# Second layer of an adaptive mixture kernel: the last four blocks in two sets of two, low-rank stages between shared experts, routed gates behind the fold product

## The chip, the cores and the metric

The kernel runs on one core of a Trainium2 chip. Its engines work side by side and wait for each other by semaphores: TensorE (PE) multiplies matrices into PSUM, VectorE (DVE) does elementwise work, ScalarE (ACT) does activation functions, GpSimd (POOL) here only memsets and broadcasts, SyncE (SP) issues DMAs. PEld is TensorE's loading of weights. The metric is the device time of one execution in microseconds, the lower the better. The kernel before takes 972.35 us (median of three runs, 971.81 to 973.3).

## The reference

Input `x` is 32 batches of 128 tokens of width 128, all in fp32. Two layers follow, each of the form `x = x + ffn(cond(x))`. Layer 0 (a mixture of four conditioned experts, then eight gated experts of width 512) is not touched here. Layer 1 is:

```
shared = sum_e (silu(x s_w1[e]) * (x s_w3[e])) s_w2[e] / 2          # 2 experts, width 256
s      = sigmoid([x, cond] W_router);  the two highest get gates, normalized
routed = sum_e gelu(x r_w1[e]) r_w2[e] * gate[:, e]                 # 8 experts, width 128, exact gelu
c      = (shared + routed) / 4
x      = x + gelu_tanh((c U1) V1 + b1) (U2 V2) + b2                 # rank 32, width 512
```

Only `c U1` of rank 32 is needed of `c`. The kernel therefore multiplies `s_w2` and `r_w2` with `U1` once, into twelve matrices of 128x32 called `fold` (with the factors 1/8 and 1/4), and never forms `c`.

## The kernel before

Tokens lie in 8 blocks of 512 (`TB`), with the 128 features on the partitions (`xT`, in layer 1 `x1T`). Layer 1 takes the blocks in two halves of four (`sb` 0 and 1, `SB = 4`). Its work is a list of units, each with an up and a down function:

- `("s", sb, k)`, four per half, one for each 128 columns of the shared experts: `sh_up` makes a gate and an up product per block (`by_columns`, line 233, in four column strips of 32), a silu on ACT (line 639) and a multiply on DVE (line 640); `sh_down` adds the fold product.
- `("r", sb, e)`, eight per half: `r_up` spreads the gate of expert e over the partitions on POOL (`spread`, line 634), makes the product `ur` per block, a gelu (line 873) and the multiply with the gate (line 874); `r_down` adds the fold product.
- `("l", sb, c)`, four per half: `low_up` multiplies the 32 rows of `pT` with 128 columns of `V1` (line 891, four row strips of 32, one per block) and takes the tanh gelu with bias (line 892); `low_down` multiplies with `U2`.

`into` (line 838) does the fold and `U2` products: block j of four goes into partitions 32 j to 32 j + 31 of one PSUM tile, so that four products with 32 columns of weights run side by side in column strips. All shared and routed folds of a half add up in one PSUM tile, `p_ps`; `low_in` copies it to `pT` (line 882). `low_out` copies `q_ps` (line 902), multiplies with `V2` (line 906), adds bias and `x1T` on DVE (line 908) and stores blocks in turn through the queues of SP and ACT (line 910).

PSUM has six rotating matmul buffers (`mm_tile`) and two for sums (`y_tile`), each one tile of 128x512 fp32. A `work` buffer `h` with three copies holds the activated values of a unit.

`pipelined` sets the order of the program: the up function of the next unit comes ahead of the down function of the present one, and `after` adds side work behind certain units. In the list, all eight s units come first, then the r units of the first half, two r units of the second half, the first three l units of the first half, the other six r units, the last l unit of the first half, and the four l units of the second half. The framework that builds the kernel may still move instructions of an engine against the program's order where it takes them to be ready earlier; waits and buffers are placed by it.

The router's gates of four blocks are transposed and go through DRAM (`gates_to_dram`, the transpose at line 555). `gate_rows` (line 863) reads them back into one partition in 32, 4 DMAs of 16 KB per half, from where POOL broadcasts.

Of the kernel before, what the change touches and what calls it, by code (L numbers as in the profile page):

```python
# [32 lines left out]
F32 = mybir.dt.float32  # L33
I32 = mybir.dt.int32
AF = mybir.ActivationFunctionType
ALU = mybir.AluOpType
AX = mybir.AxisListType

P = 128
B, S, D = 32, 128, 128  # L40
BB = 4
TB = BB * S
NB = B // BB
SB = 4
NS = NB // SB
NT = B * S // P
H = 512
NC = H // P
E0, EF, E1 = 4, 8, 8
# [43 lines left out]
AT32, NCOLS32 = columns(COLS32)  # L93
# [5 lines left out]
def adaln_ffn(  # L99
# [3 lines left out]
    nc = tc.nc  # L103
    V = nc.vector

    cpool = ctx.enter_context(tc.tile_pool(name="const", bufs=1))
    wpool = ctx.enter_context(tc.tile_pool(name="weights", bufs=1))
    apool = ctx.enter_context(tc.tile_pool(name="acts", bufs=1))
    work = ctx.enter_context(tc.tile_pool(name="work", bufs=2))
# [3 lines left out]
    def mm_tile(name):  # L113
        return psum.tile([P, TB], F32, tag="mm", name=name, bufs=6)

    def y_tile(name):
        return psum.tile([P, TB], F32, tag="y", name=name, bufs=2)

    def const(shape, name, dtype=F32):
        return cpool.tile(shape, dtype, tag=name, name=name)  # L120
# [3 lines left out]
    par32 = const([P, NCOLS32], "par32")  # L124
    rows = const([P, NROW], "rows")
# [11 lines left out]
    ident = const([P, P], "ident")  # L137
# [17 lines left out]
    for to, w in zip(downs_t, (s_w2, r_w2[: E1 // 2], r_w2[E1 // 2 :])):  # L155
        n = w.shape[0]
        nc.sync.dma_start(out=to.rearrange("p (e f) -> p e f", e=n), in_=w.rearrange("e d f -> d e f"))

    def col(name, i=0, n=1):
        return par[:, AT[name].start + i : AT[name].start + i + n]  # L160
# [67 lines left out]
    def by_columns(ps, w, x, n):  # L228


        for at in range(0, P, n):
            own = slice(at, at + n)
            nc.tensor.matmul(ps[own, :], lhsT=w[:, own], rhs=x, start=True, stop=True)  # L233

# [307 lines left out]
    def of_sb(t, sb):  # L544

        return t[:, sb * SB * BB : (sb + 1) * SB * BB, :]
# [4 lines left out]
    def gates_to_dram(kind, sb):  # L551

        gates, name = held.pop((kind, sb)), f"{kind}g{sb}"
        ps = mm_tile(f"{name}_ps")
        nc.tensor.transpose(ps[:, :P], gates.rearrange("p e b -> p (e b)"), ident)
        t = work.tile([P, P], F32, tag="gsb", name=f"{name}_sb", bufs=1)
        V.tensor_copy(t, ps[:, :P])
        d = dram.tile([P, P], F32, tag=name, name=name)
        nc.sync.dma_start(out=d, in_=t)
        in_dram[kind, sb] = d.rearrange("(g k b) t -> k g (b t)", g=2, k=4)  # L560

    def ffn_logits(sb):

# [31 lines left out]
    def fetch_rows(blk):  # L595

        sb, j = divmod(blk, SB)
        t = work.tile([P, 2, TB], F32, tag="gT", name=f"fgT{blk}")
        for k in range(4):
            nc.sync.dma_start(  # L600
                out=t[32 * k : 32 * k + 1, :, :], in_=in_dram["f", sb][k : k + 1, :, j * TB : (j + 1) * TB]
            )
        return t

# [26 lines left out]
    def spread(row, name):  # L631

        bc = work.tile([P, TB], F32, tag="bc", name=name, bufs=4)
        nc.gpsimd.partition_broadcast(bc, row)  # L634
        return bc

    def glu(ps_gate, ps_up, h, name):
        s = work.tile([P, TB], F32, tag="sg", name=name, bufs=4)
        nc.scalar.activation(s, ps_gate, AF.Silu)  # L639
        V.tensor_tensor(h, s, ps_up, ALU.mult)  # L640

    l1 = const([P, NT, E1], "l1")

# [126 lines left out]
    def l1_scores(sb):  # L770
        at = split(of_sb(l1, sb))
        V.tensor_tensor(at, logits("l1", par[:, AT["r1x"]], xT, sb)[:, :, :, :E1], split(of_sb(tl, sb)), ALU.add)
        nc.scalar.activation(of_sb(l1, sb), of_sb(l1, sb), AF.Sigmoid)

    def after_ffn(blk, e):

# [53 lines left out]

    low_p = {}

    def into(y, w, h, first, last):

        for j in range(SB):
            nc.tensor.matmul(y[32 * j : 32 * (j + 1), :], lhsT=w, rhs=h[:, j, :], start=first, stop=last)  # L838

    def sh_up(sb, k):  # L840
        e, c = divmod(k, 2)
        h = work.tile([P, SB, TB], F32, tag="h", name=f"hs_{sb}_{k}", bufs=3)
        for j in range(SB):
            x = x1T[SB * sb + j]
            g, u = mm_tile(f"g1_{sb}_{k}_{j}"), mm_tile(f"u1_{sb}_{k}_{j}")
            by_columns(g, sws_t[0][:, e, c, :], x, 32)
            by_columns(u, sws_t[1][:, e, c, :], x, 32)
            glu(g, u, h[:, j, :], f"s1_{sb}_{k}_{j}")
        return h

    def sh_down(sb, k, h):
        if k == 0:
            low_p[sb] = y_tile(f"p_ps{sb}")
        into(low_p[sb], fold[:, k, :], h, k == 0, False)


    grows = [
        wpool.tile([P, 2, SB * TB], F32, tag=tag, name=f"grows{sb}") for sb, tag in enumerate(("wg", "wu"))
    ]

    def gate_rows(sb):
        for k in range(4):
            nc.sync.dma_start(out=grows[sb][32 * k : 32 * k + 1, :, :], in_=in_dram["r", sb][k : k + 1, :, :])

    def r_up(sb, e):
        h = work.tile([P, SB, TB], F32, tag="h", name=f"hr_{sb}_{e}", bufs=3)
        g, k = divmod(e, 4)
        for j in range(SB):
            gate = spread(grows[sb][32 * k : 32 * k + 1, g, j * TB : (j + 1) * TB], f"rg_{sb}_{e}_{j}")
            ps = mm_tile(f"ur_{sb}_{e}_{j}")  # L870
            by_columns(ps, rw1_t[:, e, :], x1T[SB * sb + j], 32)
            a = work.tile([P, TB], F32, tag="sg", name=f"ar_{sb}_{e}_{j}", bufs=4)
            nc.scalar.activation(a, ps, AF.Gelu)  # L873
            V.tensor_tensor(h[:, j, :], a, gate, ALU.mult)  # L874
        return h

    def r_down(sb, e, h):
        into(low_p[sb], fold[:, 2 * 2 + e, :], h, False, e == E1 - 1)

    def low_in(sb):  # L880
        t = work.tile([P, TB], F32, tag="pT", name=f"pT{sb}", bufs=1)
        V.tensor_copy(t, low_p[sb])
        held["p", sb] = t

    def low_up(sb, c):
        h = work.tile([P, SB, TB], F32, tag="h", name=f"hl_{sb}_{c}", bufs=3)
        at = AT32["v1"].start + c * P
        for j in range(SB):
            ps = mm_tile(f"ul_{sb}_{c}_{j}")
            own = slice(32 * j, 32 * (j + 1))  # L890
            nc.tensor.matmul(ps, lhsT=par32[own, at : at + P], rhs=held["p", sb][own, :], start=True, stop=True)  # L891
            nc.scalar.activation(h[:, j, :], ps, AF.Gelu_apprx_tanh, bias=col("b1", c))
        return h

    def low_down(sb, c, h):
        if c == 0:
            held["q", sb] = y_tile(f"q_ps{sb}")
        into(held["q", sb], col("u2", c * 32, 32), h, c == 0, c == NC - 1)

    def low_out(sb):  # L900
        q = work.tile([P, TB], F32, tag="lgT", name=f"qT{sb}", bufs=1)
        V.tensor_copy(q, held["q", sb])
        for j in range(SB):
            ps = mm_tile(f"o_ps{sb}_{j}")
            own = slice(32 * j, 32 * (j + 1))
            nc.tensor.matmul(ps, lhsT=par32[own, AT32["v2"]], rhs=q[own, :], start=True, stop=True)  # L906
            t = work.tile([P, TB], F32, tag="fin", name=f"fin{sb}_{j}", bufs=4)
            V.scalar_tensor_tensor(t, ps, col("b2"), x1T[SB * sb + j], ALU.add, ALU.add)
            queue = nc.sync if j % 2 == 0 else nc.scalar
            queue.dma_start(out=out[SB * sb + j], in_=t)  # L910


    STAGES = {"f": (ffn_up, ffn_down), "s": (sh_up, sh_down), "r": (r_up, r_down), "l": (low_up, low_down)}
    units = [("f", blk, e) for blk, e in ffn_units]
    units += [("s", sb, k) for sb in range(NS) for k in range(4)]
    units += [("r", 0, e) for e in range(E1)]
    units += [("r", 1, 0), ("r", 1, 1)]
    units += [("l", 0, c) for c in range(NC - 1)]
    units += [("r", 1, e) for e in range(2, E1)]

    units += [("l", 0, NC - 1)]
    units += [("l", 1, c) for c in range(NC)]

    def after(kind, sb, i):
        if kind == "f":
            after_ffn(sb, i)
        if (kind, sb, i) == ("s", 0, 0):
            gate_rows(0)
            while rest:
                rest.pop(0)()  # L930

        if (kind, sb, i) == ("s", 0, 1):
            logits_ahead("l1", par[:, AT["r1x"]], xT, 1)
        if (kind, sb, i) == ("s", 0, 2):
            l1_scores(1)
        if (kind, sb, i) == ("s", 0, 3):
            route(1)
        if (kind, sb, i) == ("s", 1, 1):
            gates_to_dram("r", 1)
            gate_rows(1)  # L940
        if kind == "r" and i == E1 - 1:
            low_in(sb)
        if (kind, sb, i) == ("l", 0, NC - 1):
            low_out(0)

    def unit_up(kind, *at):
        return STAGES[kind][0](*at)
# [2 lines left out]
        STAGES[kind][1](*at)  # L950

    pipelined(units, unit_up, unit_down, after)
    low_out(1)


# [77 lines left out]
```

## Time and profile before

The profiled execution took 972.82 us, of which the span is 971.0 us.

| stage of the span, us | what runs | PE busy | ACT busy | DVE busy | POOL busy |
|---|---|---|---|---|---|
| 802.00 to 812.50 | first s unit and the end of layer 0 | 10.50 | 2.97 | 5.00 | 3.09 |
| 812.50 to 868.60 | s units of both halves, router of the second | 56.10 | 22.22 | 32.04 | 0.00 |
| 868.60 to 911.60 | ten r units | 43.00 | 24.41 | 36.03 | 39.43 |
| 911.60 to 918.50 | first three l units of the first half | 6.90 | 6.87 | 1.46 | 2.78 |
| 918.50 to 944.40 | six r units of the second half | 25.90 | 16.87 | 22.41 | 21.47 |
| 944.40 to 965.20 | five l units, both outputs | 19.61 | 13.13 | 6.29 | 0.00 |
| 965.20 to 971.00 | last sums and stores | 0.00 | 0.00 | 2.69 | 0.00 |

In the profile a line of a time line gives start, duration, engine, source line, operation, output and inputs, shapes, a count of merged instructions, and in brackets the idle time ahead with what ended it. An fp32 matmul has two records, so x8 stands for four matmuls. Where a matmul's start waits on one strip, the records of the strips beside it go on, so busy time of PE includes some waiting.

### The profile page before, as it was taken

To read this page: it belongs to the slowest core of one execution; us is meant where nothing else is said; L and a number is where in the kernel's file an instruction comes from. 1 tells how busy PE (TensorE), PEld (TensorE's weight loads), DVE (VectorE), ACT (ScalarE), POOL (GpSimd) and SP (SyncE) were. 2 spreads that over 40 slices of the span, in tenths; PEclk is the share of its full clock that TensorE was granted. 3 is DMA by queue.
4 is the path that set the end of the run, shared out by engine and by line. 5 is a ranking of instruction groups with operands and counts; after the bars stand their busy time and mean duration, and the time that the engine had idled before them with its cause. 6 is when DMAs were issued, how large, how long until landed. Compare 5 with 4: busy or idle time off the path is not lost.

```text
span 971.0 us, 15510 instructions
## 1 busy us (share of the span) xinstructions
PE 957.0 (99%) x5966; PEld 446.9 (46%) x5966; DVE 630.1 (65%) x1130; ACT 345.0 (36%) x615; POOL 142.4 (15%) x150
## 2 busy tenths in 40 slices
PE   7999999999999999999999999999999999999997
PEld 3588984444444444444444444444444443333342
DVE  3444565767866776685676887567667655648593
ACT  5455544223322322232232332223223223335764
POOL 0000001210101011010101011010100001009680
PEclk9999999999999999999999999999999999999999
DMA  9745650000000000000000000000000000000002
GB/s 319 237 133 154 209 187 24 5 1 4 1 1 1 1 1 1 1 1 1 1 2 1 1 2 4 1 1 1 1 1 1 1 2 2 2 7 1 1 2 87
DMA packets 19043, 34.05 MB, mean 35 GB/s; under 512 B 1729, under 2 KB 9921, under 8 KB 18945
## 3 DMA queue, kind: packets, MB, share of 16 engines
q1 hardware_dynamic: 18096, 31.43, 10.6%
q10 hardware_dynamic: 864, 1.52, 0.4%
q8 instruction: 52, 0.85, 0.4%
q14 instruction: 31, 0.25, 0.1%
HBM read 30.59 MB, written 2.36 MB: 34 GB/s over the span
## 4 chain that ended last, share of the span: by engine, by line
PE 85%; DVE 0%; DVEq 0%; issue 0%
PE g L233 26%; PE u L233 25%; PE ya L721 11%; PE yb L721 9%; PE ur L233 6%; PE p_ps L838 2%; PE ul L891 1%; PE us L257 1%; PE ys L268 1%; PE q_ps L838 1%; PE y L510 0%; PE u L494 0%; PE fold_ps L244 0%; PE o_ps L906 0%; PE lg_ps L526 0%; PE l_ps L526 0%
## 5 line engine op out<-in xcount | busy, mean ns | idle before, releaser
L639 ACT ACTIVATE sf<-g 128x512 f32<-128x512 f32 x256 | 152.7, 597 | 435.2 <-PE g L233 421.3
L640 DVE TENSOR_TENSOR hf<-sf,u 128x512 f32<-128x512 f32 x256 | 174.8, 685 | 183.2 <-PE u L233 182.1
L233 PE MATMUL g<-c0all,wg_t 128*64 128x512 f32 x1024 | 263.5, 593 | 0.0
L233 PE MATMUL u<-cg,wu_t 128*64 128x512 f32 x1024 | 263.1, 592 | 0.0
L634 POOL PARTITION_BROADCAST fg<-fgT x64 | 72.4, 1140 | 657.5 <-DVE cg L682 494.4
L233 PEld LDWEIGHTS u<-cg,wu_t 128*64 128x64 f32 x1024 | 73.6, 137 | 146.2 <-issue 127.6
L233 PEld LDWEIGHTS g<-c0all,wg_t 128*64 128x64 f32 x1024 | 72.9, 137 | 121.3 <-issue 107.1
L721 PE MATMUL ya<-t,wd_t 128*64 128x256 f32 x512 | 121.0, 379 | 0.0
L634 POOL PARTITION_BROADCAST rg<-grows x64 | 67.6, 1184 | 143.8 <-DVE hr L874 75.5
L874 DVE TENSOR_TENSOR hr<-ar,rg 128x512 f32<-128x512 f32 x64 | 60.7, 995 | 15.9 <-ACT ar L873 15.9
L721 PEld LDWEIGHTS ya<-t,wd_t 128*64 128x64 f32 x512 | 70.1, 137 | 0.0
L497 ACT ACTIVATE h<-u,w 128x256 f32<-128x256 f32 (+3 forms) x136 | 50.3, 429 | 54.3 <-PE u L494 54.3
L721 PE MATMUL yb<-hf,a_sum 128*64 128x256 f32 x512 | 66.1, 379 | 0.0
L721 PE MATMUL ya<-hf,wd_t 128*64 128x256 f32 x256 | 65.8, 379 | 0.0
L721 PE MATMUL ya<-t,a_sum 128*64 128x256 f32 x256 | 65.7, 379 | 0.0
L701 DVE TENSOR_TENSOR hf<-hf 128x512 f32<-128x512 f32 x64 | 63.0, 984 | 2.2
L233 PE MATMUL ur<-xall,rw_t 128*32 128x512 f32 x512 | 58.4, 592 | 0.0
L721 PEld LDWEIGHTS ya<-hf,wd_t 128*64 128x64 f32 x256 | 35.0, 137 | 46.1 <-issue 36.8
L510 PE MATMUL y<-h,w 128*128 128x256 f32 (+3 forms) x272 | 53.1, 338 | 1.0 <-DVE t L513 1.0
L494 PE MATMUL u<-x,w 128*128 128x256 f32 (+3 forms) x272 | 53.0, 338 | 1.1 <-DVEq L475 1.1
L494 PEld LDWEIGHTS u<-x,w 128*128 128x128 f32 x272 | 45.3, 190 | 5.7 <-ACT h L497 1.3
L873 ACT ACTIVATE ar<-ur 128x512 f32<-128x512 f32 x64 | 37.9, 598 | 27.6 <-PE ur L233 27.3
(211 smaller groups left out, 918.6 us busy)
## 6 DMA issues: line engine op xcount, KB each, us to landing
w<-in_experts SPq DMA_DIRECT2D x36, 514.5 KB
xall<-in_x SPq DMA_DIRECT2D x8, 256.0 KB
wg_t<-in_w_gate SPq DMA_DIRECT2D x8, 256.0 KB
wu_t<-in_w_up SPq DMA_DIRECT2D x8, 256.0 KB
wd_t<-in_w_down SPq DMA_DIRECT2D x8, 256.0 KB
out<-fin SPq DMA_DIRECT2D x4, 256.0 KB
out<-fin ACTq DMA_DIRECT2D x4, 256.0 KB
downs<-in_r_w SPq DMA_DIRECT2D x2, 256.0 KB
```

Of the source, the lines that this page charges most:

```text
L233: nc.tensor.matmul(ps[own, :], lhsT=w[:, own], rhs=x, start=True, stop=True)
L494: nc.tensor.matmul(ps[c][:, :m, :n], lhsT=w1, rhs=x[:, :m, :n], start=True, stop=True)
L497: nc.scalar.activation(h[:, c, :m, :n], ps[c][:, :m, :n], AF.Gelu_apprx_tanh, bias=bias)
L510: nc.tensor.matmul(y[:, :m, :n], lhsT=w2, rhs=h[:, c, :m, :n], start=(c == 0), stop=(c == NC - 1))
L634: nc.gpsimd.partition_broadcast(bc, row)
L639: nc.scalar.activation(s, ps_gate, AF.Silu)
L640: V.tensor_tensor(h, s, ps_up, ALU.mult)
L701: V.tensor_tensor(b12, b12, b11, ALU.subtract)
L721: nc.tensor.matmul(y[half, n], lhsT=w[:, c, :], rhs=h[:, c, :], start=first, stop=(e == EF - 1 and last))
L838: nc.tensor.matmul(y[32 * j : 32 * (j + 1), :], lhsT=w, rhs=h[:, j, :], start=first, stop=last)
L873: nc.scalar.activation(a, ps, AF.Gelu)
L874: V.tensor_tensor(h[:, j, :], a, gate, ALU.mult)
```

## The change

It touches layer 1 alone.

- The blocks now form three groups: blocks 0 to 3 in four strips of 512 tokens as before, blocks 4 and 5, and blocks 6 and 7. A group of two blocks is cut into four strips of 256 tokens for the folds and the low-rank stages; the shared and routed up-products keep 512 columns.
- A routed unit of a group of two takes two experts. The gate is no longer multiplied into the activated values. The fold product of one expert goes into a PSUM tile of its own (one half of a tile for each of the two experts), DVE multiplies it with the gate and adds it to `low_p` in SBUF, which begins as the copy of the shared experts' sum.
- The gates come by DMA from DRAM already broadcast to 32 partitions per strip, for all eight experts (`gate_rows`: 4 DMAs of 512 KB and 8 of 256 KB); POOL broadcasts nothing more in layer 1.
- New order: s and r units of group 0; for group 1 s, s, l, l, s, s, l, l with the l units of group 0, then its four r units; the same for group 2 with the l units of group 1; then an empty unit and the l units of group 2. The output of a group comes behind the first r unit of the next.
- Matmuls in strips of 32 and ACT's instructions of layer 1 are pinned behind the instruction that the program has ahead of them on their engine. `table` issues a 1x1 activation that loads the next function's table.
- The last output: for the odd strips `x1T` is added by an identity product, issued ahead, and ACT adds the bias; DVE takes the even strips. Four stores of 128x256 follow, three on SP and one on ACT.
- The gate transpose and `gate_rows` of the second half come behind the second r unit; the sigmoid of the second half's router comes behind the last silu of group 0.

```diff
             own = slice(at, at + n)
-            nc.tensor.matmul(ps[own, :], lhsT=w[:, own], rhs=x, start=True, stop=True)
+            mm = nc.tensor.matmul(ps[own, :], lhsT=w[:, own], rhs=x, start=True, stop=True)
+            if n < 64:
+                tc.keep_in_program_order(mm)
...
+    GROUPS = ((0, 4, TB), (4, 2, TB // 2), (6, 2, TB // 2))
+    def in_order(inst):
+        tc.keep_in_program_order(inst)
+    tiny = const([1, 1], "tiny")
+    def table(func):
+        if held.get("table") != func:
+            in_order(nc.scalar.activation(tiny, ones[:1, :1], func))
+            held["table"] = func
...
+    def into(y, w, strips, first, last):
+        for j, h in enumerate(strips):
+            in_order(nc.tensor.matmul(y[32 * j : 32 * (j + 1)], lhsT=w, rhs=h, start=first, stop=last))
+    def strips_of(h, group):
+        n = GROUPS[group][2]
+        return [h[:, b, at : at + n] for b in range(h.shape[1]) for at in range(0, TB, n)]
...
+    def sh_down(group, k, h):
+        _, n, size = GROUPS[group]
+        if k == 0:
+            held["shared", group] = y_tile(f"p_ps{group}")[:, :size]
+        y = held["shared", group]
+        into(y, fold[:, k, :], strips_of(h[:, :n, :], group), k == 0, k == 3)
+        if k == 3:
+            low_p[group] = work.tile([P, 2, TB], F32, tag="gT", name=f"pT{group}")[:, 0, :size]
+            V.tensor_copy(low_p[group], y)
...
     def gate_rows(sb):
-        for k in range(4):
-            nc.sync.dma_start(out=grows[sb][32 * k : 32 * k + 1, :, :], in_=in_dram["r", sb][k : k + 1, :, :])
+        rows = in_dram["r", sb]
+        for group in (0,) if sb == 0 else (1, 2):
+            n = GROUPS[group][2]
+            for j in range(SB):
+                at = (max(group, 1) - 1) * SB * n + j * n
+                to = gates_t[sb][32 * j : 32 * (j + 1)]
+                if group > 0:
+                    to = to.rearrange("p e (g t) -> p e g t", g=2)[:, :, group - 1, :]
+                nc.sync.dma_start(out=to, in_=rows[:, at : at + n].partition_broadcast(32))
+    def r_up(group, i):
+        table(AF.Gelu)
+        h = work.tile([P, SB, TB], F32, tag="h", name=f"hr_{group}_{i}", bufs=3)
+        pieces = [(e, b) for e in experts_of(group, i) for b in blocks(group)]
+        for at, (e, b) in enumerate(pieces):
+            ps = mm_tile(f"ur_{b}_{e}")
+            by_columns(ps, rw1_t[:, e, :], x1T[b], 32)
+            in_order(nc.scalar.activation(h[:, at, :], ps, AF.Gelu))
+        return h
+    def r_down(group, i, h):
+        _, n, size = GROUPS[group]
+        ys = y_tile(f"py_{group}_{i}")
+        for at, e in enumerate(experts_of(group, i)):
+            own = h[:, at * n : (at + 1) * n, :]
+            y = ys[:, at * size : (at + 1) * size]
+            into(y, fold[:, 2 * 2 + e, :], strips_of(own, group), True, True)
+            t = work.tile([P, TB], F32, tag="sg", name=f"pg_{group}_{e}", bufs=4)[:, :size]
+            V.tensor_tensor(t, y, gate_of_strips(e, group), ALU.mult)
+            V.tensor_tensor(low_p[group], low_p[group], t, ALU.add)
+    def by_rows(ps, w, t, j, first=True):
+        own = slice(32 * j, 32 * (j + 1))
+        in_order(nc.tensor.matmul(ps, lhsT=par32[own, w], rhs=t[own, :], start=first, stop=True))
...
+    def out_begin():
+        for j in (1, 3):
+            b, at = strip(2, j)
+            held["o", j] = mm_tile(f"o_x{b}")[:, : TB // 2]
+            in_order(nc.tensor.matmul(held["o", j], lhsT=ident, rhs=x1T[b][:, at], start=True, stop=False))
+    def out_end():
+        fins = {b: work.tile([P, TB], F32, tag="fin", name=f"fin{b}", bufs=4) for b in blocks(2)}
         for j in range(SB):
+            b, at = strip(2, j)
+            t = fins[b][:, at]
+            ps = held["o", j] if j % 2 else mm_tile(f"o_ps{b}")[:, : TB // 2]
+            by_rows(ps, AT32["v2"], held["qT", 2], j, first=j % 2 == 0)
+            if j % 2 == 0:
+                V.scalar_tensor_tensor(t, ps, col("b2"), x1T[b][:, at], ALU.add, ALU.add)
+            else:
+                in_order(nc.scalar.activation(t, ps, AF.Identity, bias=col("b2")))
+        for j in (0, 2, 3, 1):
+            b, at = strip(2, j)
+            queue = nc.scalar if j == 1 else nc.sync
+            queue.dma_start(out=out[b][:, at], in_=fins[b][:, at])
...
+    units += [("s", 0, k) for k in range(4)] + [("r", 0, e) for e in range(E1)]
+    for group in (1, 2):
+        s, l = [("s", group, k) for k in range(4)], [("l", group - 1, c) for c in range(NC)]
+        units += s[:2] + l[:2] + s[2:] + l[2:] + [("r", group, i) for i in range(E1 // 2)]
+    units += [("-", 0, 0)] + [("l", 2, c) for c in range(NC)]
...
         if (kind, sb, i) == ("s", 0, 2):
+            table(AF.Sigmoid)
             l1_scores(1)
         if (kind, sb, i) == ("s", 0, 3):
             route(1)
-        if (kind, sb, i) == ("s", 1, 1):
+        if (kind, sb, i) == ("r", 0, 1):
             gates_to_dram("r", 1)
             gate_rows(1)
-        if kind == "r" and i == E1 - 1:
-            low_in(sb)
-        if (kind, sb, i) == ("l", 0, NC - 1):
-            low_out(0)
+        if kind == "l" and i == NC - 1:
+            low_q(sb)
+        if kind == "r" and sb > 0 and i == 0:
+            low_out(sb - 1)
+        if (kind, sb, i) == ("l", 2, 2):
+            out_begin()
```

`sh_up`, `low_up`, `low_down` and `low_out` change in the same way: groups for halves, strips for blocks, `table` at the start of an up function and `in_order` around matmuls and activations. `low_up` of a group of two works on 256 columns.

## The prediction

> **What bounds the kernel now.** I read the page's sums first, then busy time by stage of the second layer, the chain that ended last, and the time line of the two places where the chain leaves TensorE.
>
> ```profile
> span 971.0 us, 15510 instructions
> ...
> PE 957.0 (99%) x5966; PEld 446.9 (46%) x5966; DVE 630.1 (65%) x1130; ACT 345.0 (36%) x615; POOL 142.4 (15%) x150
> ...
> PEclk9999999999999999999999999999999999999999
> ```
>
> TensorE (PE) is the bound at full clock; VectorE (DVE), ScalarE (ACT) and GpSimd (POOL) matter only where PE waits. Stages, as PE, PEld, DVE, ACT, POOL busy, granted clock, DMA:
>
> ```profile
> 868.60:911.60 43.00, 43.00 (x404) 12.87 (x396) 36.03 (x41) 24.41 (x42) 39.43 (x38) 1.00 0.01 2
> 911.60:918.50 6.90, 6.90 (x52) 2.23 (x52) 1.46 (x2) 6.87 (x11) 2.78 (x3) 1.00 0.00 0
> 918.50:944.40 25.90, 25.90 (x244) 12.69 (x236) 22.41 (x22) 16.87 (x29) 21.47 (x20) 1.00 0.01 2
> 944.40:965.20 20.80, 19.61 (x108) 5.68 (x104) 6.29 (x11) 13.13 (x21) 0.00 (x0) 1.00 0.14 51
> ```
>
> PE looks busy everywhere, but a waiting matmul counts as busy. Count matmuls instead: 404 in 43 us against 108 in 20.8. The unit is T, one 128x128 weight applied to 512 tokens: in the chain below four take 3.43, so T = 0.857. Routed experts run at T; the low-rank stages do not.
>
> ```profile
> 907.40 3.43 PE ur L233 x32
> 910.84 0.86 PE p_ps L838 x8
> 911.69 1.07 PE ul L891 x8
> 912.76 1.40 PE p_ps L838 x8
> 914.16 1.09 PE ul L891 x8
> 915.25 1.08 PE q_ps L838 x8
> ...
> 946.99 0.70 DVE pT L882
> 947.69 0.04 issue
> 947.74 1.14 PE ul L891 x8
> ...
> 959.79 3.45 PE q_ps L838 x15
> 963.24 0.03 issue
> 963.26 0.70 DVE qT L902
> ```
>
> What to see: a change between column strips (L838) and row strips (L891) costs 1.08 - 0.86 = 0.22. Why the tail is slow stands in ACT's time line:
>
> ```profile
> 911.52 1.28 ACT L892 ACT_TABLE_LOAD   x1
> 912.81 7.17 ACT L892 ACTIVATE hl<-ul,par 128x512 f32<-128x512 f32 x12
> ...
> 953.32 1.67 ACTq L910 DMA_DIRECT2D out<-fin  x2
> 955.04 7.09 ACT L892 ACTIVATE hl<-ul,par 128x512 f32<-128x512 f32 x12 [3.72 <-DVE fin L908]
> ```
>
> ACT spends 0.58 on each 512-wide gelu and stood 3.72 behind its own output DMAs, which wait for VectorE's sums. From the end of the last routed up-product (PE's next matmul starts at 943.39) to the span's end are 27.6 us, for 14 T = 12.0 of matmuls.
>
> **The change, part by part**, against the profiled execution (span 971.0, its own time 972.82, so 1.82 around the span; it lies 0.47 above the median, so I add 1.35 to a span to compare with the median).
>
> *Matmul work* is unchanged: a 256-token product takes half. The layer-0 down products of 256 columns start in pairs every 0.215 (799.22, 799.43, 799.65), half of the 0.43 at 512.
>
> *Tail.* After it, only the last group's folds, low rank and output follow the last routed up-product: 2 + 4 + 0.5 = 6.5 T, so 7.5 T = +6.4 move ahead of that point, E. From E: group 2's last two fold units with their eight 256-wide DVE operations (0.41 each by L247, 414 ns for 128x256 out of PSUM) end at E + 4.8. From DVE's end to the first gelu was 1.22 (947.68 to 948.90) with a 0.86 matmul inside; now 0.79. Sixteen gelus of 256: four took 1.77 at L497 with PE pacing them, 512-wide ones 0.58 less 0.21 for the columns gives 0.37; I take 0.40, so 6.4, ending at E + 12.0. Last gelu to copy was 1.13, now 0.70; copy 0.42; product 0.79; two half-wide sums 0.9; from the last sum to the end before 3.06 (967.94 to 971.0), plus 0.2 as SP now issues three of four at some 0.58 each. E + 18.1; bounds 16.5 and 19.5 (0.37 or 0.43 per gelu, half a microsecond; a microsecond either way for landing). Against 27.6: -9.5. The two early identity products fall into PE's idle time there: nothing (at 0.43 each if not).
>
> *Low rank amid shared experts.* Before, the l stages of the first half lost 918.50 - 911.62 - 6 T = 1.74, and 0.2 behind them: -1.9, since they go. After there are four such places: two pairs of l units beside group 1's shared units and two beside group 2's. Each runs up, fold, up, down with four mode changes, and its second up needs banks that the first's gelus hold. The nearest row is the same passage of before: from the first ul (911.62) to the third (916.26) 4.64 for four products. With a half-wide fold in it, 4.64 - 3.5 T = 1.64. With the 256-wide l units of group 1 it starts later against ACT: the table load begins when the last silu ends, about PE's end of the s unit; plus 1.3 and about 0.2 for the tiny activation; then four gelus. Counting from the first ul (0.43 later): 1.07 + 3 x 0.39 + 0.48 + 0.55 = 3.27, less 2 T = 1.56. Sum 2 x 1.64 + 2 x 1.56 = +6.4. Bounds: mode changes alone 4 x 0.88 = 3.5; a whole gelu train exposed, 2.5 each, 10. I take the middle, since its row has the same order of waits.
>
> [...] The table switch in the trace is 1.28, and the next gelu starts 1.31 after the last ended (911.50 to 912.81). [...]
>
> *Output products of groups 0 and 1* now stand amid routed units: two mode changes of 0.22 each, +0.9 for both; between 0 and 1.8 (waits for banks). Their sums and stores lie beside routed units, where DVE has half of its time.
>
> *Gates behind the fold.* 64 broadcasts on POOL and 64 multiplies (L874, 60.7) go; 24 multiplies and 24 adds come (0.69 at 512, 0.41 at 256): 11 + 13 us of DVE. PE set the pace before, so that gains nothing directly. But in groups 1 and 2 each routed unit folds two experts into two halves of one 512-wide PSUM tile, with the first half's multiply issued between them. If the second fold has to wait for that read: from the first's nominal end 0.22 to DVE's start (record 0.18 late, 0.04), 0.41, then 0.06 and some 0.13 of weight load: 0.83 of PE standing, as the next routed matmuls are pinned behind it. Six units before E: +5.0 (the last two are in the tail; 0.6 there). No row of before shows PE writing a tile that is being read: each reader follows all writers. Bounds: 0 without the wait; 1.24 per unit, 7.4, if DVE has an add ahead of the multiply. I take 0.83: it is one tile in one buffer, and the round trip p_ps to pT to ul is the nearest row.
>
> [...]
>
> *Moved steps that I cost at nothing.* Gate rows: 4 + 8 DMAs broadcast into 32 partitions, 2 MB per half, 0.58 of SP issue each, nothing queued behind on SP but stores much later. They wait for layer 0's last read of its weights (about 809) and are needed at about 845: 36 us against 16 at the slowest early slice (133 GB/s); the second half has some 50. Uncovered, PE would stand for the difference. The gate transpose for blocks 4 to 7 moves from after the second s unit of the second half to after r(0,1), about 850; PE's following routed matmuls are queued behind it. The router's DVE chain from 838.05 sums to some 9.1 by its rows (five of 1.22 and twelve small ones) and ends near 847 to 849. Cover: 1 to 2 us, its cost if gone. Tables loaded ahead in the r and s units lie beside 3.4 us of matmuls.
>
> Sum: -9.5 + 6.4 - 1.9 + 6.4 + 0.9 + 5.0 = **+7.3**: span 978.3, time 979.6.
>
> **Rivals.**
> *A, no bank wait.* The second fold runs through. For it: the halves share no address. [...] -5.6 (5.0 and the 0.6 in the tail): +1.7, time 974.0, at the edge of no change.
> *B, faster: the middle runs at T.* One mechanism: PE's pinned stream never stands between 870 and E, because the six matmul banks and the table loads issued ahead let gelus and multiplies drain beside the next shared or routed products. For it: two shared and two low-rank units are 13 T = 11.1 us of PE, and need about 10 of ACT. Against: 911.6 to 918.5, where the same order did stall. The losses 6.4 + 0.9 + 5.0 + 0.6 go: -5.6, time 966.7. It decides below 3.7 us of losses in the middle.
> *C, ACT becomes the bound of the l places.* Of the 10 us of ACT per 11.1 of PE at 512 (8 gelus 4.7, two table loads with their tiny activations 3.0, four silus 2.4) all comes in one order: little slack. If each place loses 2.5 (+3.6) and the folds find DVE busy (+2.4): +13.3, time 985.6.
>
> **How the numbers follow.** What this kernel's measurement can tell is 0.2%, 1.9 us. Forecast 0.57, A 0.14, B 0.19, C 0.10. A splits about evenly between same and slower, B gives 0.15 faster and 0.04 same, and 0.01 of the forecast's low end is same: faster 0.15, same 0.12, slower 0.73. The lower bounds of the terms sum to -3.1 and the upper to +15.6; the range leaves out B's faster part and the far end of C: 971 to 986. The forecast's own range is 976 to 983.
>
> **What would show it.** Right: from E to the end about 18.1, ACT without the 3.72 gap; PE's matmuls between the two folds of one routed unit about 1.25 apart instead of 0.43, with PEld waiting for DVE; about 4.6 and 3.3 from the first ul of a pair to the next s unit; table loads near 24 instead of 17. Wrong: folds of one unit back to back (A); ul pairs without waits on ACT (B); PE waiting for gate rows or for the gate transpose, or matmuls of 256 columns in four strips not at half cost, which no row of before shows for 32 columns.

## The result and the profile after

The changed kernel takes 981.17 us (median of six runs, 980.14 to 982.00) against 972.73 beside it (six runs, 971.81 to 973.30): 1.0088 times the time before, 95% interval 1.0078 to 1.0099. The change makes it slower by 8.4 us; the forecast was 979.6, 7.3 slower.

The page of the profiled execution (981.42 us, of which the span is 979.6):

```profile
span 979.6 us, 15727 instructions
...
PE 961.2 (98%) x6138; PEld 453.9 (46%) x6138; DVE 593.8 (61%) x1118; ACT 358.6 (37%) x654; POOL 74.8 (8%) x86
...
PEclk9999999999999999999999999999999999999998
```

VectorE lost 36 us of work and GpSimd 68, and none of it is time gained. New is the last digit of the clock row, an 8. Busy time by stage of the second layer, columns as before (PE, PEld, DVE, ACT, POOL, granted clock, DMA):

```profile
870.80:904.00 33.20, 33.20 (x303) 13.87 (x299) 9.30 (x14) 24.99 (x41) 0.00 (x0) 1.00 0.00 1
904.00:923.00 19.00, 16.35 (x176) 5.66 (x172) 9.72 (x20) 8.69 (x15) 0.00 (x0) 1.00 0.15 56
923.00:946.00 23.00, 23.00 (x246) 11.29 (x249) 6.05 (x11) 17.00 (x35) 0.00 (x0) 1.00 0.01 1
...
963.00:976.00 13.00, 10.50 (x80) 4.35 (x76) 1.95 (x5) 6.65 (x17) 0.00 (x0) 0.74 0.00 1
```

The first and third rows are shared units with pairs of l units among them: PE counts as busy throughout. The second holds the routed units of the first set of two, with 2.65 us in which PE does nothing at all; before, no stretch of routed units had any. The last is the end of the tail, at a mean clock of 0.74. The three places one by one, first a pair of l units of the second set of two in the chain that ended last:

```profile
938.13 0.64 PE ul L943 x8
938.77 0.57 PE p_ps L865 x8
939.34 1.10 PE ul L943 x8
940.45 0.64 PE q_ps L865 x8
941.09 3.43 PE ur L233 x32
```

Four products of half width, 2 T = 1.71 of work, take 2.77 in PE's own time line (938.06 to 940.83; 2.80 in the pair before). For the pairs of 512 columns here is that time line:

```profile
879.40 1.28 ACT L855 ACT_TABLE_LOAD   x1
...
879.94 1.14 PE L943 MATMUL ul<-pT,par 32*128 32x512 f32 x8
...
881.10 4.74 ACT L953 ACTIVATE hl<-ul,par 128x512 f32<-128x512 f32 x8 [0.20 <-PE ul L943]
...
883.47 1.15 PE L865 MATMUL q_ps<-hl,par 128*32 128x512 f32 x8
...
884.35 1.13 PE L233 MATMUL g<-xall,sws 128*32 128x512 f32 x8
```

From the first `ul` (879.94) to the next shared product (884.35) are 4.41 where the work is 3.5 T = 3.0; the other pair also takes 4.41 (892.71 to 897.12). ACT waits only 0.20 after the table load, since the load began while PE was still on the shared unit. Now the folds of one routed unit, in the same view:

```profile
911.25 0.61 PE L865 MATMUL py<-hr,fold 128*32 128x256 f32 x8
...
911.93 0.42 DVE L937 TENSOR_TENSOR pg<-py,gates 128x256 f32<-128x256 f32 x1 [1.32 <-PE py L865]
...
912.41 0.64 PE L865 MATMUL py<-hr,fold 128*32 128x256 f32 x8 [0.55 <-DVE pg L937]
```

The second fold starts 1.16 after the first instead of 0.43, and its bracket names the multiply of the first half: PE stands until DVE has read. The six units ahead of the tail show 1.31, 1.16, 1.25, 1.51, 1.29 and 1.16 (at 1.51 DVE comes late, from a multiply of the shared unit). Last, the tail: PE's first fold behind the last routed product, which is E, its first `ul` of the last set, and ACT's gelus:

```profile
959.15 0.61 PE L865 MATMUL py<-hr,fold 128*32 128x256 f32 x8
...
964.09 1.13 PE L943 MATMUL ul<-pT,par 32*128 32x256 f32 x12 [0.99 <-DVE pT L938]
964.88 3.03 ACT L953 ACTIVATE hl<-ul,par 128x256 f32<-128x256 f32 x8 [3.37 <-PE ul L943]
...
969.25 1.57 ACT L953 ACTIVATE hl<-ul,par 128x256 f32<-128x256 f32 x4 [1.33 <-PE ul L943]
...
971.43 1.57 ACT L953 ACTIVATE hl<-ul,par 128x256 f32<-128x256 f32 x4 [0.61 <-PE ul L943]
```

The 3.72 in which ACT stood behind its output stores are gone, as forecast, but two new waits on PE stand in the train of gelus, 1.33 and 0.61. Busy time, over the four microseconds from 960 and then by single ones, says why:

```profile
960.00:964.00 4.00, 1.71 (x24) 0.68 (x24) 3.10 (x8) 1.49 (x2) 0.00 (x0) 1.00 0.00 0
...
965.00:966.00 1.00, 0.81 (x7) 0.59 (x4) 0.00 (x0) 1.00 (x4) 0.00 (x0) 0.67 0.06 16
966.00:967.00 1.00, 1.00 (x8) 0.35 (x10) 0.00 (x0) 1.00 (x4) 0.00 (x0) 0.50 0.00 0
...
972.00:973.00 1.00, 1.00 (x7) 0.68 (x4) 0.00 (x0) 1.00 (x3) 0.00 (x0) 0.91 0.00 0
```

From 960 to 964 PE works 1.71 us of 4, as it waits for the last folds' multiplies. Some 1.3 us after it has work again its granted clock falls to 0.50 and stays there, with PE fully busy, until about 972: the change from `ul` to the fold and back then takes 2.18 per l unit (966.92 to 969.10) and PE paces ACT.

Against the span before (971.0, so +8.6), with E as in the prediction (959.15 here, forecast 960.2). The moved work and the old losses are reckoned from rows of before in both columns; the rest is read from the trace:

| part | forecast | measured |
|---|---|---|
| tail, E to the end (20.4 against 27.6) | -9.5 | -7.2 |
| work moved ahead of E, 7.5 T | +6.4 | +6.4 |
| losses of the old l stages, gone | -1.9 | -1.9 |
| four pairs of l units, 2 x 1.41 + 2 x 1.07 | +6.4 | +5.0 |
| outputs of groups 0 and 1, 0.35 each | +0.9 | +0.7 |
| six fold waits, the intervals above less 0.43 each | +5.0 | +5.1 |
| left over | | +0.5 |

The 0.5 need not be a step of the change. Kernels that are the same up to E (the runs below) differ there by as much: 943.39, 943.05 and 942.62 for the kernel before, 959.15, 959.33 and 958.73 for the change.

### The profile page after: what moved, and what is told of

Its sections match the earlier page's. It is cut to its first block, busy times and chain, and to the rows that moved or that the text cites. A ratio compares the mean times of both kernels' runs of the same rounds, so it can differ in the third digit from the quotient of the medians.

```text
span 979.6 us, 15727 instructions
## 1 busy us (share of the span) xinstructions
PE 961.2 (98%) x6138; PEld 453.9 (46%) x6138; DVE 593.8 (61%) x1118; ACT 358.6 (37%) x654; POOL 74.8 (8%) x86
## 4 chain that ended last, share of the span: by engine, by line
PE 85%; DVE 1%; issue 0%; ACT 0%; ACTq 0%; DVEq 0%
PE g L233 25%; PE u L233 25%; PE ya L725 11%; PE yb L725 8%; PE ur L233 6%; PE py L865 2%; PE ul L943 1%; PE us L259 1%; PE ys L270 1%; PE q_ps L865 1%; PE p_ps L865 1%; DVE pg L937 0%; PE y L512 0%; PE u L496 0%; PE fold_ps L246 0%; PE o_ps L943 0%
## 5 line engine op out<-in xcount | busy, mean ns | idle before, releaser
L926 ACT ACTIVATE hr<-ur 128x512 f32<-128x512 f32 x64 | 37.2, 593 | 29.2 <-PE ur L233 29.2
L512 PEld LDWEIGHTS y<-h,w 128*128 128x128 f32 x272 | 44.9, 190 | 4.7 <-issue 0.8
L686 DVE TENSOR_TENSOR cg<-c0all,fg 128x512 f32<-128x512 f32 x64 | 44.9, 702 | 1.8 <-POOL fg L637 1.8
```

The costliest lines, as they stand in the source:

```text
L512: nc.tensor.matmul(y[:, :m, :n], lhsT=w2, rhs=h[:, c, :m, :n], start=(c == 0), stop=(c == NC - 1))
L686: V.tensor_tensor(t, c0T[blk], bcast.pop(i), ALU.mult)
L926: in_order(nc.scalar.activation(h[:, at, :], ps, AF.Gelu))
```

## The experiments

Two things were to be settled: whether the middle's losses are the folds' shared tile and the pairs (the forecast's theory) or ACT and its table loads (rival C), and what the clock does to the tail. Each ratio is to the kernel before, run on the same chip.

**Both folds of a unit ahead of the multiplies.** In `r_down` of the changed kernel:

```diff
         for at, e in enumerate(experts_of(group, i)):
             own = h[:, at * n : (at + 1) * n, :]
             y = ys[:, at * size : (at + 1) * size]
             into(y, fold[:, 2 * 2 + e, :], strips_of(own, group), True, True)
+        for at, e in enumerate(experts_of(group, i)):
+            y = ys[:, at * size : (at + 1) * size]
             t = work.tile([P, TB], F32, tag="sg", name=f"pg_{group}_{e}", bufs=4)[:, :size]
```

> Both folds of a routed unit of groups 1 and 2 are issued ahead of the two multiplies; the tile stays one. If the second fold waits because the multiply reads the other half of its tile, the two folds now start 0.43 apart instead of 1.16 to 1.51, the six waits before E (5.1 in the changed kernel's trace) go, and about 0.6 to 1 more in the tail: 975.3, between 974.5 and 976. If the waits come from DVE being late or from the pinned order as such, the time stays near 981.

**A tile of its own for each expert**, with the order left alone:

```diff
-        ys = y_tile(f"py_{group}_{i}")
...
-            y = ys[:, at * size : (at + 1) * size]
+            y = y_tile(f"py_{group}_{e}")[:, :size]
```

> The program's order stays (fold, multiply, add, fold, multiply, add); each expert's fold gets a tile of its own of the two for sums. If sharing the tile makes the wait, the result is that of both folds ahead, about 975.3. If it is the order of the program (the multiply between the folds, everything pinned), the time stays near 981. If the two buffers now run short, a wait for the add of the unit before appears instead, 0.4 to 0.9 per unit.

Measured: 974.62 us, 1.0022 times before (1.0013 to 1.0032), and 973.92, 1.0018 (1.0008 to 1.0027). Against the change's 1.0088 either edit is worth 0.66 to 0.70%, 6.4 to 6.8 us. The time line of the first now shows the two folds as one run of 16 records, without a bracket:

```profile
910.20 1.05 PE L865 MATMUL py<-hr,fold 128*32 128x256 f32 x16
...
910.45 0.60 ACT L926 ACTIVATE hr<-ur 128x512 f32<-128x512 f32 x1 [0.26 <-PE ur L233]
```

Neither edit changes the number or size of the instructions, and the second not even their order, so the wait was the sharing of one tile between a write and a read. E comes 5.3 us earlier in the first (953.86) and 5.7 in the second (953.46), where the six waits added up to 5.1. The waits are placed by the framework; what the chip does with the two accesses without this one was not tried.

The profiled execution of the second, at 972.59 us, is also the change without either of its two losses: the clock stayed full until PE's last product (granted 1.00 in all rows from 952 to 968), with no product added, and ACT's gelus run in one train (time line).

```profile
953.46 1.05 PE L865 MATMUL py<-hr,fold 128*32 128x256 f32 x16
...
957.47 1.13 PE L942 MATMUL ul<-pT,par 32*128 32x256 f32 x12 [1.32 <-DVE pT L937]
...
958.26 6.00 ACT L952 ACTIVATE hl<-ul,par 128x256 f32<-128x256 f32 x16 [2.44 <-PE ul L942]
```

Its span is 970.8 (971.0 before), and its tail from E to the end 17.3.

**The clock of the tail.** The changed kernel with unread identity products where PE waits for the last multiplies, one between the folds of the third unit of the last set, two in the fourth, two behind it:

```diff
             into(y, fold[:, 2 * 2 + e, :], strips_of(own, group), True, True)
+            if group == 2 and i >= 2 and at == 0:
+                keep_busy(f"warm{i}", i - 1)
...
+    def keep_busy(name, times):
+        ps = mm_tile(name)[:, : TB // 2]
+        for _ in range(times):
+            in_order(nc.tensor.matmul(ps, lhsT=ident, rhs=x1T[6][:, : TB // 2], start=True, stop=True))
...
+        if (kind, sb, i) == ("r", 2, 3):
+            keep_busy("warm_end", 2)
```

> Five 256-wide products whose result nobody reads are put where PE stands still behind E: one and two between the folds of the last two routed units, two behind the last fold. If the tail is 2.3 longer than forecast because the granted clock falls to 0.50 at 965 after PE stood idle, the clock stays at 1.00 and the time falls by 1.5 to 2.3, to about 979. If ACT's gelus or the waits for buffers set the tail, the time stays near 981 or rises by the products' own 0.5 or so.

Measured: 978.78 us, 1.0065 (1.0048 to 1.0082), 0.23% or 2.2 us under the change. More work for PE made the kernel faster. ACT's sixteen gelus run without a gap (time line), and the clock is full in the stretch in which it was half (busy time by stage):

```profile
964.47 5.99 ACT L960 ACTIVATE hl<-ul,par 128x256 f32<-128x256 f32 x16 [3.38 <-PE ul L950]
```

```profile
960.00:964.00 4.00, 3.97 (x37) 2.17 (x41) 2.76 (x7) 1.08 (x2) 0.00 (x0) 1.00 0.00 0
964.00:968.00 4.00, 3.84 (x40) 1.98 (x35) 0.00 (x0) 3.53 (x10) 0.00 (x0) 1.00 0.02 4
```

The last gelu ends at E + 11.7 and the span at E + 18.3 (E is 958.73, the span 977.0), where the forecast had 12.0 and 18.1. So 2.2 of the tail's 2.3 us beyond the forecast went with the clock.

**One set of four instead of two of two.** The changed kernel with `GROUPS = ((0, 4, TB), (4, 4, TB))`, one expert per routed unit, the last l units and output at 512 columns:

```diff
-    GROUPS = ((0, 4, TB), (4, 2, TB // 2), (6, 2, TB // 2))
+    GROUPS = ((0, 4, TB), (4, 4, TB))
...
-        return (i,) if group == 0 else (2 * i, 2 * i + 1)
+        return (i,)
...
-    out_end()
+    low_out(1)
```

> The last four blocks stay one group of 512-token strips; the interleaving of the first group's low-rank units, the gates behind the fold, the pins and the table loads stay; the last output goes as that of the other groups, with all sums on DVE. By the terms: no tile is shared by two experts, so no waits between folds; two pairs cost 1.4 each and the first output 0.4; the tail is about 22.8 from E with 3 T moved ahead of it: 1 us below before, about 971.7, between 970 and 974. If the interleaving is what costs, it stays above 976.

Measured: 974.05 us, 1.0016 (1.0006 to 1.0026). The expected number was missed by 2.3. PE now waits 2.02 at once for the gate multiplies and adds of the last unit (time line), and the clock falls (busy time by stage):

```profile
950.71 4.61 PE L936 MATMUL ul<-pT,par 32*128 32x512 f32 x16 [2.02 <-DVE pT L931]
...
959.27 4.73 ACT L946 ACTIVATE hl<-ul,par 128x512 f32<-128x512 f32 x8 [2.60 <-PE ul L936]
```

```profile
951.00:953.00 2.00, 2.00 (x13) 0.74 (x10) 0.00 (x0) 1.07 (x2) 0.00 (x0) 0.80 0.00 0
953.00:955.00 2.00, 2.00 (x6) 0.66 (x3) 0.00 (x0) 2.00 (x5) 0.00 (x0) 0.50 0.00 0
955.00:960.00 5.00, 5.00 (x25) 0.88 (x24) 0.00 (x0) 2.40 (x5) 0.00 (x0) 0.60 0.00 0
```

The tail is 25.9 from E (946.75 to 972.7) where 22.8 were expected, with 6.8 us of it at half rate, in which ACT waits 2.60 for a `ul`. That the clock is the cause is argued from these lines; this kernel was not run with the clock held up. One set of four, whose folds share no tile either, stands where the two sets stand once their folds no longer wait (1.0018 and 1.0022): these runs show no gain from the cut into two sets.

**The gates alone.** The kernel before, at 512 columns, with the routed gates behind the fold product:

```diff
-            a = work.tile([P, TB], F32, tag="sg", name=f"ar_{sb}_{e}_{j}", bufs=4)
-            nc.scalar.activation(a, ps, AF.Gelu)
-            V.tensor_tensor(h[:, j, :], a, gate, ALU.mult)
+            nc.scalar.activation(h[:, j, :], ps, AF.Gelu)
...
-        into(low_p[sb], fold[:, 2 * 2 + e, :], h, False, e == E1 - 1)
+        y = y_tile(f"py_{sb}_{e}")
+        into(y, fold[:, 2 * 2 + e, :], h, True, True)
+        t = work.tile([P, TB], F32, tag="sg", name=f"pg_{sb}_{e}", bufs=4)
+        V.tensor_tensor(t, y, gates_t[sb][:, e, :], ALU.mult)
+        V.tensor_tensor(held["p", sb], held["p", sb], t, ALU.add)
```

> The kernel before with one part of the change alone: gates broadcast by DMA and applied behind the fold, one expert per tile, 512 tokens wide; order of the units, halves and outputs as before. DVE and POOL are relieved of 64 multiplies and 64 broadcasts. PE set the pace there, so nothing is gained; the tail has one DVE operation more between the last fold and the first low-rank product: +0.7, about 972.8, between 972 and 974. If the relief of DVE and POOL were worth something, it would fall below 971; if the 4 MB of gate rows disturbed PE, it would rise above 975.

Measured: 973.69 us, 1.0015 (1.0005 to 1.0024). The page shows the relief, 39 us of DVE and 68 of POOL, for nothing:

```profile
PE 957.8 (99%) x5966; PEld 447.2 (46%) x5966; DVE 591.1 (61%) x1098; ACT 345.1 (35%) x615; POOL 74.8 (8%) x86
```

PE set the pace of the routed units already. Behind the last routed product two steps of DVE (multiply and add, 0.69 each) stand where one copy stood, and from E to the end are 28.1 (944.12 to 972.2) against 27.6. The rest of the 1.4 us is not explained.

**Fewer table loads.** The changed kernel with all four shared units of a set first and the four l units behind them in a row, which leaves four of the eight table loads at these places:

```diff
-        units += s[:2] + l[:2] + s[2:] + l[2:] + [("r", group, i) for i in range(E1 // 2)]
+        units += s + l + [("r", group, i) for i in range(E1 // 2)]
```

> The changed kernel with the low-rank units four in a row behind the four shared units, so two pairs of table loads fewer in each of groups 1 and 2. If the loss of these places comes from the second unit's products waiting for buffers and the next fold waiting for the last gelu, four in a row lose 2.7 (512 wide) and 3.0 (256 wide) against 2.8 and 2.1 for two pairs: 982, between 980.5 and 983. [...]

Measured: 979.99 us, 1.0080 (1.0063 to 1.0097), a little below the range expected without a saving by fewer loads, and far above the 976 that a saving of 1.28 for each of four loads would have given (981.17 - 5.12). In the time line of the first place, PE's first `ul`, the gelus and the next routed product:

```profile
888.17 1.14 PE L943 MATMUL ul<-pT,par 32*128 32x512 f32 x8
...
889.33 9.41 ACT L953 ACTIVATE hl<-ul,par 128x512 f32<-128x512 f32 x16 [0.20 <-PE ul L943]
...
897.21 2.32 PE L233 MATMUL ur<-xall,rw_t 128*32 128x512 f32 x19
```

Eight products of 7.5 T = 6.4 take 9.04, a loss of 2.6 against 2.8 for two pairs; the place of 256 columns (935.18 to 940.86, 4 T = 3.4) loses 2.25 against 2.1. Half the loads, the same loss. The longer train of gelus could hide a saving in that sum, but the lines rule it out: the first gelu starts 1.16 after the first `ul` here (888.17 to 889.33) and in the change, and 1.16 also in the tail of before, where no load stands ahead of it (947.74 to 948.90). At 256 columns it is 0.83 to 0.86, against 0.79 without a load in the change's tail. So the loads are all but hidden, and what is left to hold PE is the train of gelus and the mode changes (0.22 for one in the rows of before). E is 959.19 against 959.15; the 1.2 us gained in the profiled spans lie behind it, in the clock (busy time by stage):

```profile
966.00:968.00 2.00, 2.00 (x15) 0.74 (x18) 0.00 (x0) 1.96 (x6) 0.00 (x0) 0.57 0.00 0
968.00:970.00 2.00, 2.00 (x20) 0.54 (x20) 0.00 (x0) 1.11 (x4) 0.00 (x0) 0.58 0.00 0
970.00:972.00 2.00, 2.00 (x20) 0.99 (x16) 0.00 (x0) 1.91 (x6) 0.00 (x0) 1.00 0.00 0
```

The low stretch lasts about 3.4 us here (2 x 0.43 / 0.5 + 2 x 0.42 / 0.5) and 6.8 in the change.

**Both causes away.** The changed kernel with a tile for each expert, four unread products behind the last unit, and the last stores all through SP:

```diff
-            y = ys[:, at * size : (at + 1) * size]
+            y = y_tile(f"py_{group}_{e}")[:, :size]
...
-            queue = nc.scalar if j == 1 else nc.sync
+            queue = nc.sync
...
+        if (kind, sb, i) == ("r", 2, 3):
+            keep_busy("warm_end", 4)
```

> The changed kernel with a tile of its own for each expert's fold, four unread 256-wide products behind the last fold, and all four last stores on SP behind the last sums. By the terms as measured (tail 18.1 less 0.6 and 0.5, no waits between folds, the pairs 5.0, the outputs 0.7): 971 to 972 with the clock at 1.00 in the tail, so no gain over before. If the clock still falls, 973.5 and more.

Measured: 973.73 us, 1.0014 (1.0004 to 1.0024), within the intervals no better than the own tile alone; the expected 971 to 972 was missed. The clock stays full until PE's last product (granted 1.00 in all rows from 945 to 968), but the unread products are too many: they hold PE until after the sum is there (time line).

```profile
956.80 1.99 PE L942 MATMUL warm_end<-xall,ident 128*128 128x256 f32 x8
...
957.27 0.87 DVE L937 TENSOR_TENSOR pT<-pT,pg 128x256 f32<-128x256 f32 x2
958.73 1.13 PE L947 MATMUL ul<-pT,par 32*128 32x256 f32 x12
```

DVE's last add ends at 958.14 and `ul` starts 0.59 later; with the own tile alone it started at 957.47, 0.05 after the add. The expectation also counted on the stores to save 0.5, where a fourth store on SP costs some 0.4 (next run). The tail is 18.3 (954.19 to 972.5) against 17.3 with the own tile alone.

**The stores.** In the changed kernel ACT's store stands between its two last sums. Moved to SP:

```diff
-        for j in (0, 2, 3, 1):
+        for j in (0, 1, 2, 3):
...
-            queue = nc.scalar if j == 1 else nc.sync
+            queue = nc.sync
```

> The changed kernel with all four last stores issued by SP, in the order of the blocks. In its trace ACT's own store (975.87, 0.37) stands between ACT's two sums (975.36 and 976.34), and the last sum ends at 976.81. Theory: that store sits on the path that sets the end; without it the second sum begins near 975.83 and the span is 0.4 to 0.5 shorter: time 980.7 against 981.2. Rival: the end is set by SP, which issues four stores of about 0.45 instead of three behind the first sum: no change, 981.2.

Measured: 982.02 us, 1.0099 (1.0084 to 1.0115): no gain. The sums do run together, and SP ends later for it (time line of this kernel):

```profile
975.49 0.84 ACT L1005 ACTIVATE fin<-o_x,par 128x256 f32<-128x256 f32 x2 [2.30 <-PE o_x L943]
975.96 1.80 SPq L1009 DMA_DIRECT2D out<-fin  x4
```

SP's last issue ends at 977.76 and the span 2.4 later; in the change SP's three ended at 977.18, and the span also 2.4 later. The rival held: the end follows SP's last issue, which a fourth store (0.45 per issue) puts later.

In the kernel before, ACT's idle 3.72 came from its share of the first half's stores. All stores through SP there:

```diff
-            queue = nc.sync if j % 2 == 0 else nc.scalar
-            queue.dma_start(out=out[SB * sb + j], in_=t)
+            nc.sync.dma_start(out=out[SB * sb + j], in_=t)
```

> The kernel before with one line changed: all stores on SP, so that ACT does not stand behind its own stores (3.72 in the tail of before). The gelus of the next unit can start as their products come; these are held by buffers that the output sums free, the last near 954.5, so 2.2 of the 3.7 come back: about 969.9, between 968.5 and 971. If ACT's standing there is hidden by the wait for those buffers, the time stays at 972.

Measured: 971.77 us, 0.9994 (0.9985 to 1.0004), about a fifth of what was expected and not told from no change. In the time line the gap is not closed but replaced:

```profile
951.98 2.46 ACT L892 ACTIVATE hl<-ul,par 128x512 f32<-128x512 f32 x4 [1.42 <-PE ul L891]
...
955.85 4.74 ACT L892 ACTIVATE hl<-ul,par 128x512 f32<-128x512 f32 x8 [1.41 <-PE ul L891]
```

Once ACT is free of its stores it waits twice, 1.4 each, for PE, which issues the next `ul` only behind the fold of the gelus before (the fold at 953.64, the `ul` at 954.63). From E to the end are 26.8 (942.62 to 969.4) against 27.6.

On top of that, the change's last output in the kernel before: identity products ahead, half of the last sums on ACT:

```diff
+            on_act = sb == 1 and j % 2 == 1
+            ps = held["o", j] if on_act else mm_tile(f"o_ps{sb}_{j}")
...
+            if on_act:
+                nc.scalar.activation(t, ps, AF.Identity, bias=col("b2"))
```

> The kernel before, with one idea of the changed kernel alone: two identity products ahead of the last output product, ACT adds the bias for the odd blocks of the last output, SP stores the even blocks, ACT the odd ones behind both of its sums; all earlier stores by SP. With the stores alone moved to SP the median was 971.77 and the four sums on DVE took 963.63 to 966.36, the stores ended at 969.4. Theory A: the sums set the end; two on each engine take 1.4 instead of 2.73 and the end comes 0.9 to 1.3 earlier: 970.5 to 970.9. Theory B: the transfers set it: 1 MB at 380 GB/s is 2.8 us, which from the first issue at 964.4 with about 1 us to start already reaches 968.2: at most 0.5 earlier, 971.3. Theory C: the identity products (0.86 each) fall between ACT's last gelus and hold them up by as much: 972 to 973.

Measured: 972.29 us, 0.9999 (0.9990 to 1.0009). The identity products (959.71, 1.98 in the time line) fall between the last folds: from the start of ACT's last train of eight gelus to the copy of `q_ps` are 6.58 (956.26 to 962.84) where the stores alone left 5.87 (955.85 to 961.72). From that copy on both need 7.7. Theory C explains the first; whether transfers or sums set the end stays open, since ACT's first store was again issued between its two sums:

```profile
965.50 0.39 ACTq L919 DMA_DIRECT2D out<-fin  x1
966.02 0.69 ACT L911 ACTIVATE fin<-o_x,par 128x512 f32<-128x512 f32 x1 [0.55 <-DVE fin L913]
```

No version here beats the kernel before by more than it can be measured.

## Why the prediction was right, and where its terms were off

The sign, the order of the terms and the mechanism held. The time came out 1.6 us above the forecast; in spans, which the table splits, it is 1.3. That it is no more is partly luck: the tail lost 2.3 more than forecast and the pairs of l units 1.4 less, two errors that have nothing to do with each other.

- **Tail, -9.5 forecast, -7.2 measured.** Steps up to the first gelu came out: `low_p` whole at E + 4.9 (forecast 4.8), first gelu at E + 5.7 (forecast 5.6). The step that failed is "I take 0.40, so 6.4, ending at E + 12.0": the last gelu ended at E + 13.85. It took the rates of rows with a full clock, and never asked what the stretch before it, with PE more than half idle behind the folds' multiplies, does to the clock. With the clock held up by unread products the last gelu ends at E + 11.7 and the tail is 18.3. Also, the prediction put the old tail's slowness down to ACT's 3.72 behind its own stores; the kernel before with these stores moved measured 0.5 us less, not told from no change, as PE's waits took their place. No term of the sum rested on that reading.
- **Fold waits, +5.0 forecast, +5.1 measured.** The 0.83 for a round trip from PE to DVE and back measured 0.73 to 1.08. Taking the shared tile away gave back 6.4 to 6.8 us in the ratios. In the profiled executions that is 5.3 and 5.7 ahead of E, 0.9 in the tail (the first `ul` of the last set at E + 4.0 instead of 4.9; forecast 0.6), and a half-rate stretch of 3.4 us in the first and none in the second, instead of 6.8.
- **Pairs of l units, +6.4 forecast, +5.0 measured.** 1.41 for 1.64 at 512 columns and 1.07 for 1.56 at 256. At 512 the load begins 0.54 ahead of the first `ul`, and ACT waits only 0.20 more behind it. At 256 every step of the forecast's chain was a little long: first `ul` to first gelu 0.86 (forecast 1.07), four gelus 1.48 (1.65), the fold behind them 0.46 (0.55).
- **Outputs, +0.9 forecast, +0.7 measured; moved work and old losses as forecast.** Two mode changes of 0.22 per output, forecast from one row of before, measured 0.35 together.
- **Table loads.** 24 loads of 1.28 against 17, as forecast. In the change a load (871.68), the tiny activation (872.97) and the next silu (873.08) follow each other within 1.40 us. The pairs came out 1.4 lower than the forecast, and with half of the loads they lose as much (2.6 and 2.25 against 2.8 and 2.1).
- **Steps costed at nothing.** The broadcast gate rows and the later gate transpose left no wait of PE in the profile, and the relief of DVE and GpSimd was worth nothing, as the kernel with the gates alone shows by itself.

Of the rivals, A (no wait at the shared tile) fell with the brackets of the second folds. Its price, 5.6 lower, was close: without the wait 6.2 to 6.6 are gone from the profiled spans ahead of and behind E, and the clock's part on top. B (the middle at rate T) needed less than 3.7 us of losses there; 10.8 were measured (5.0 + 0.7 + 5.1). C (ACT the bound) needed 2.5 per place; the places lost 1.41 and 1.07, and fewer table loads changed nothing.

Without both the fold waits and the low clock the tail is 17.3 (profiled execution with the own tile), 10.3 less than before, and the sum is -10.3 + 6.4 - 1.9 + 5.0 + 0.7 = -0.1. That execution's span is 0.2 below that of before, which is no change: the shorter tail is paid for by the work and the mode changes moved ahead of it. The kernel built to have both away measured +1.4 (1.0014), 0.6 of it by its own unread products and some 0.4 by the fourth store on SP.

## What to carry to other kernels

Here the cut of the last set in two shortened the serial tail only by what then had to run elsewhere: count the moved work at its full price and each added pass through a small stage with its mode changes, before the details decide. Two results in one PSUM tile with a read between their writes made the writer wait for the reader, 0.73 to 1.08 us each time; put both writes first, or give each its own tile. Before pricing a tail by rows from a busy stage, look at how dense TensorE's work is in the microseconds ahead of it, since the clock that was granted there need not last: in the change PE worked 1.71 us of 4, and the clock then fell from 1.00 to 0.50.

## What the runs showed of the hardware

In the change TensorE's clock fell to half although PE was never idle for longer than 1.0 us. It worked 1.71 us of the 4 from 960 to 964, and the fall came at about 965.3, when PE was busy again. The half-rate stretches last 6.8 us in the change (0.66 + 6 + 0.18, from the clocks of 0.67, 0.50 and 0.91) and in the kernel with one set of four (0.8 + 2.0 + 4.0), and 3.4 with the l units in a row and in the kernel with both folds first, whose busy time by stage reads:

```profile
960.00:964.00 4.00, 4.00 (x34) 1.47 (x32) 0.00 (x0) 3.19 (x9) 0.00 (x0) 0.57 0.00 0
964.00:966.00 2.00, 2.00 (x23) 0.95 (x18) 0.00 (x0) 1.69 (x5) 0.00 (x0) 1.00 0.00 0
```

Why these stretches come to 3.4 and to 6.8 us was not measured. How long the clock stays low seems to differ from run to run: ten runs of the kernel with both folds first go from 972.37 us at a mean clock of 1.000 over 973.09 at 0.998 to 974.00 to 975.94 at 0.996 to 0.997, and those of the own tile from 972.59 at 1.000 to 974.27 to 975.18 at 0.996, while all six of the change have 0.996. This mean counts the time behind PE's last product too, where the clock also falls: the profile with both causes away has 0.998, and its clock is 1.00 until PE is done at 967.7 and 0.50 from 969 to 972. How little work of PE brings the clock down was not measured.
